# A four-layer graph kernel on one core: the end of layer 1 by quarters of the nodes instead of halves, and another spread of the odd counts

## Chip, cores and metric

The kernel runs on one core of one Trainium2 chip. The metric is the device time of one execution in microseconds (us), the median of the runs shown.

## The reference, cut to what matters

`x` is 4096 nodes by 64 features, `adj` a 4096 x 4096 matrix of zeros and ones. Four layers follow each other, and each adds to `x` what it makes of `h`, the normalised and rectified `x`.

```python
h = jnp.maximum(_layernorm(x, axis=-1), 0.0)
x = x + _L1_gnn_ref(h, adj, ...)      # layer 1
...
# inside _L1_gnn_ref: all pairs of nodes, then work by node
support_t = jnp.einsum('ij,ijd->id', adj_att, x_local)
return proj(expmap(x, support_t, c), c)
...
# _L2_gnn_ref
h_neigh = (adj @ X + X) / deg
z = jnp.concatenate([X, h_neigh], axis=1) @ W + b
out = jax.nn.relu(z); return out / jnp.maximum(norm(out), L2_EPS)
...
# _L3_gnn_ref: the last 100 neighbours of a node, each weighted half of the next
rank = jnp.cumsum(mask, axis=1)
pos = rank - (deg - k)
w = mask * jnp.where(pos > 0, DECAY ** (k - pos), 0.0)
out = w @ (input @ weight) + bias
```

Layer 0 (graph attention with several heads) is not touched by the change.

## The kernel before, in words

**Nodes and tiles.** The 4096 nodes are 32 blocks of 128 (`NB = 32`); `x` and `h` are tiles of 128 partitions by 32 blocks by 64 features. A group is 4 blocks (`GB = 4`, 512 nodes), and there are 8 groups (`NG`). A half is 16 blocks, a quarter 8.

**Who sets the order.** The kernel is recorded through a tile layer. A planner orders the instructions of each engine's queue by costs of its own and keeps the data dependencies; every engine then works its queue strictly in order, and a wait blocks all that stands behind it. Two means pin that order. `in_order()` (lines 921 to 940) ties all instructions of VectorE, ScalarE and TensorE recorded inside it to the one recorded ahead on the same engine. `tc.issue_after(i)` lets the planner place what is recorded inside only behind instruction `i`.

**Odd counts.** `count_odd` (line 946) loads 1 MB of the adjacency into one of two `raw` buffers (SP's queue, line 949) and counts on VectorE the entries that are neither 0 nor 1 (line 950). There are 64 of these. They feed a flag that chooses the general kernel at the end, and nothing else, so they may stand anywhere; they are spread over the layers. This text calls them counts.

**Layer 1, pairs** (`pairs_fast`, from line 2130). For 36 pairs of groups, two to a batch, weights (`sg`), distances (`at`, `xt`) and their transposes (`pf`) are made, and TensorE adds up `accj` and `acci` (line 2280) in PSUM. VectorE adds each finished group to `VT` (lines 2311, 2312, 2338). The last batches are (7,0),(7,1); (7,2),(7,3); (7,4),(7,5); (7,6),(7,7): the columns of groups 0 and 1 are final three batches ahead of the end.

**Layer 1, end by node** (`finish_steps`, line 2356, then `norm_steps`, line 959, and `nodes`, line 2495). For a run of blocks TensorE turns `VT` back (`pvt`, line 2376) and VectorE scales it into `VQ` (2380). Then some 14 wide steps over nodes by 64 features (`xv`, `xu`, `xg`, `V`, ..., `hs`) and some 30 small ones over nodes alone follow on VectorE, with ScalarE between: a square (`vv`), Sqrt (`un`), Tanh (`arg`), Sqrt (`pp`), the norm's square and Sqrt, and two copies into `HH` (lines 2499, 2506), the high and low parts of `h` that layer 2 multiplies by. Sqrt and Tanh need different tables, and a table load (`ACT_TABLE_LOAD`) stands ahead of each change. The steps are Python generators: a `yield True` marks a wait for ScalarE. `side_by_side` runs half 0 and takes, at each such mark, up to two steps of half 1 (ten in all); the whole stands in `in_order`.

**Layer 2** (from line 2594). For each half `hf` of the target nodes, 8 steps `q` load 1 MB of the mask (`m2`, line 2601, three buffers); TensorE multiplies 16 times for `nacc` (line 2606, needs `HH` of four blocks) and 16 times for `dc` (line 2619, the degrees, needs no `HH`). After a half VectorE and ScalarE copy the sums out (`ev`, `cf`), and four groups go one by one through `layer2_group` (line 2546): `pnf`, `cat`, `tr`, `pz`, `zt`, `nrm`, the norm, `tr`, `psup`, `lo`. Half 1's groups run beside half 2's multiplications. Here `half 1` and `half 2` are `hf = 0` and `hf = 1`.

**Layer 3** (from line 2649). Four passes `u` of 1024 target nodes; in each, 32 blocks `j`: per block TensorE makes the ranks (`pv`, lines 2675 and 2683), ScalarE the weights as powers of two (`w3b`, line 2692), TensorE the sums (`sacc`, line 2657). Masks of 0.5 MB (`m3`, line 2668) come through SP's queue, where the counts' loads stand too. Half 2's groups of layer 2 run beside pass `u = 0`; the counts of layer 3 are held until the last of them (`valued[-1]`).

**Where the counts stand before.** 16 in layers 0 and 1; in layer 2, behind the last node step (`ready[-1]`), `q = 5, 6, 7` of half 1 and `q = 0` to `4` of half 2, that is 8; in layer 3 seven in `u = 0` and 11 in each later pass, that is 40.

Of the kernel before, what the change touches and what calls it, by code (L numbers as in the profile page):

```python
# [9 lines left out]
F32 = mybir.dt.float32  # L10
# [14 lines left out]
P = 128  # L25
N = 4096
NB = N // P
D = 64
G = 512
NG = N // G  # L30
GB = G // P
JT = 4
NQ = NB // JT
# [20 lines left out]
HB = NB // 2  # L54
# [776 lines left out]
def kernel(  # L831
# [66 lines left out]
    halves = [slice(b, b + NB // 2) for b in range(0, NB, NB // 2)]  # L898
# [57 lines left out]
    def small(name, width=NB):  # L956
        return spool.tile([P, width], F32, name=name, tag=name)

    def norm_steps(bs, wide, tag, act=True):


        nb = bs.stop - bs.start
        hb = h[:, bs]
        mean = small(f"ln_mean{nb}", nb)
        nc.vector.tensor_reduce(mean, x[:, bs], AX.X, ALU.add)
        yield False
        nc.vector.tensor_scalar(mean, mean, 1.0 / D, None, ALU.mult)
        nc.vector.tensor_tensor(hb, x[:, bs], over(mean, D), ALU.subtract)
        yield False
        sq = wide.tile([P, nb, D], F32, name="ln_sq", tag=tag)  # L970
        if act:
            nc.scalar.activation(sq, hb, AF.Square)
        else:
            nc.vector.tensor_tensor(sq, hb, hb, ALU.mult)
        yield act
        var = small(f"ln_var{nb}", nb)
        nc.vector.tensor_reduce(var, sq, AX.X, ALU.add)
        nc.scalar.activation(var, var, AF.Sqrt, bias=eps_t, scale=1.0 / D)
        yield True
        nc.vector.reciprocal(var, var)  # L980
        nc.vector.scalar_tensor_tensor(hb, hb, 0.0, over(var, D), ALU.max, ALU.mult)
        yield False

    def layernorm_relu(pool=None, tag="wide"):
        with ExitStack() as ln:
            wide = pool or ln.enter_context(tc.tile_pool(name="ln", bufs=2))
            for bs in halves:
                for _ in norm_steps(bs, wide, tag, act=pool is None):
                    pass

    def side_by_side(first, second, fill, most):


        for wait in first:
            for _ in range(min(fill, most) if wait else 0):
                next(second)
                most -= 1
        for _ in second:
            pass

    def transpose_to(dst, src, cols, pool, engine_copy):

# [40 lines left out]
    with ExitStack() as l0:  # L1043
# [260 lines left out]
        with ExitStack() as pa:  # L1304
# [3 lines left out]
            ps = pa.enter_context(tc.tile_pool(name="ps_prep", bufs=2, space=PSUM))  # L1308
# [1044 lines left out]
                if n + 2 < len(batches):  # L2353
                    distances(batches[n + 2])

    def finish_steps(hf, VQ, VT, fold_v, pabs, f, f2, kp, pf, ac2, wide, ps):

        bs = halves[hf]
        n = bs.stop - bs.start
        V, hb, ab = VQ[:, bs, 0:D], h[:, bs], a[:, bs]

        def scal(name):
            return small(name, n)

        def fat(name):
            return wide.tile([P, n, D], F32, name=name, tag="fat")  # L2370

        for g in range(hf * NG // 2, (hf + 1) * NG // 2):
            pt = ps.tile([P, GB, D1], F32, name="pvt", tag="misc")
            for b in range(GB):
                c = (g * GB + b) * P
                nc.tensor.matmul(
                    pt[:, b, :], lhsT=VT[:, c : c + P], rhs=fold_v, start=True, stop=True
                )
            gs = slice(g * GB, (g + 1) * GB)
            nc.vector.tensor_tensor(VQ[:, gs, :], pt, over(pabs[:, gs], D1), ALU.mult)  # L2380
            yield g % 2 == 0
        t = fat("xv")
        nc.vector.tensor_tensor(t, hb, V, ALU.mult)
        yield False
        xu = scal("xu")
        nc.vector.tensor_reduce(xu, t, AX.X, ALU.add)
        yield False
        g = scal("fing")
        nc.vector.scalar_tensor_tensor(g, xu, m2c, VQ[:, bs, D], ALU.mult, ALU.add)
        nc.vector.tensor_tensor(g, g, pinv[:, bs], ALU.mult)  # L2390
        t = fat("xg")
        nc.vector.tensor_tensor(t, hb, over(g, D), ALU.mult)
        yield False
        nc.vector.tensor_tensor(V, V, t, ALU.subtract)
        t = fat("vv")
        nc.scalar.activation(t, V, AF.Square)
        yield True
        nc.vector.tensor_tensor(g, g, ab, ALU.mult)
        nc.vector.tensor_tensor(xu, xu, g, ALU.subtract)
        nc.vector.tensor_tensor(xu, xu, f[:, bs], ALU.mult)  # L2400
        uu, un, arg = scal("uu"), scal("un"), scal("arg")
        nc.vector.tensor_reduce(uu, t, AX.X, ALU.add)
        nc.vector.tensor_tensor(uu, uu, f2[:, bs], ALU.mult)
        nc.vector.tensor_scalar(un, uu, MIN_NORM, None, ALU.max)
        nc.scalar.activation(un, un, AF.Sqrt)
        yield True
        nc.vector.tensor_tensor(arg, un, kp[:, bs], ALU.mult)
        nc.scalar.activation(arg, arg, AF.Tanh)
        nc.vector.reciprocal(un, un)
        yield True  # L2410

        nc.vector.scalar_tensor_tensor(arg, un, rabs, arg, ALU.mult, ALU.mult)
        nc.vector.tensor_tensor(uu, uu, arg, ALU.mult)
        nc.vector.tensor_tensor(uu, uu, arg, ALU.mult)
        nc.vector.tensor_tensor(xu, xu, arg, ALU.mult)
        num, den, one2, pp = scal("mnum"), scal("mden"), scal("one2"), scal("pp")
        nc.vector.tensor_scalar(one2, xu, p2c, 1.0, ALU.mult, ALU.add)
        nc.vector.tensor_tensor(den, ac2[:, bs], uu, ALU.mult)
        nc.vector.tensor_tensor(den, den, one2, ALU.add)
        nc.vector.tensor_scalar(den, den, MIN_NORM, None, ALU.max)  # L2420
        nc.vector.scalar_tensor_tensor(pp, xu, 2.0, ab, ALU.mult, ALU.add)
        nc.vector.tensor_tensor(pp, pp, uu, ALU.add)
        nc.vector.tensor_tensor(pp, pp, den, ALU.mult)
        nc.vector.tensor_scalar(pp, pp, 1e-36, None, ALU.max)
        nc.scalar.activation(pp, pp, AF.Sqrt)
        nc.vector.scalar_tensor_tensor(num, uu, cc, one2, ALU.mult, ALU.add)
        nc.vector.reciprocal(den, den)
        nc.vector.tensor_tensor(arg, arg, pf[:, bs], ALU.mult)
        yield True

        nc.vector.reciprocal(pp, pp)
        nc.vector.scalar_tensor_tensor(den, pp, maxn, den, ALU.mult, ALU.min)
        nc.vector.tensor_tensor(arg, arg, den, ALU.mult)
        nc.vector.tensor_tensor(num, num, den, ALU.mult)
        nc.vector.tensor_tensor(V, V, over(arg, D), ALU.mult)
        yield False
        t = fat("xn")
        nc.vector.tensor_tensor(t, hb, over(num, D), ALU.mult)
        yield False
        nc.vector.tensor_tensor(V, V, t, ALU.add)  # L2440
        yield False
        nc.vector.tensor_tensor(x[:, bs], x[:, bs], V, ALU.add)
        yield False
        yield from norm_steps(bs, wide, "fat")


    VALH = float(1 << 12)
    VBITS = 128.0

    def layers_fast(es, *sums):  # L2450
        HO2 = N // 4
        NK = HO2 // G
        cp = es.enter_context(tc.tile_pool(name="lconst", bufs=1))
# [10 lines left out]
        cnt16 = cp.tile([P, 2, G], BF16, name="cnt16")  # L2464

        ps = es.enter_context(tc.tile_pool(name="ps_l23", bufs=2, space=PSUM))
        wide = es.enter_context(tc.tile_pool(name="finwide", bufs=3))
        lp = es.enter_context(tc.tile_pool(name="l2f", bufs=1))
        work = es.enter_context(tc.tile_pool(name="l2fwork", bufs=2))
        w2 = lp.tile([2 * D, D], F32, name="w2f")  # L2470
# [21 lines left out]
        )  # L2492
        ready, valued = [], []

        def nodes(hf):
            yield from finish_steps(hf, *sums, wide, ps)
            bs = halves[hf]
            hs = wide.tile([P, HB, D], F32, name="hs", tag="fat")
            nc.scalar.activation(HH[:, bs, 0, :], h[:, bs], AF.Copy, scale=VALH)
            yield True  # L2500
            ready.append(
                nc.vector.scalar_tensor_tensor(
                    hs, h[:, bs], VALH, HH[:, bs, 0, :], ALU.mult, ALU.subtract
                )
            )
            nc.scalar.activation(HH[:, bs, 1, :], hs, AF.Copy, scale=LO)


        with in_order():
            side_by_side(nodes(0), nodes(1), 2, 10)  # L2510

        def not_before_nodes():
            return tc.issue_after(ready[-1].ins)
# [81 lines left out]
        with tc.tile_pool(name="ps_nacc", bufs=6, space=PSUM) as ps_acc:  # L2595
            for hf in range(2):
                accs = [ps_acc.tile([P, G], F32, name="nacc", tag="nacc") for _ in range(NS)]
                dc = ps_acc.tile([P, G], F32, name="dc", tag="nacc")
                for q in range(NQ):
# [3 lines left out]
                    for t in range(JT):  # L2603
                        j = q * JT + t
                        for k in range(NS):
# [4 lines left out]
                                start=(j == 0),  # L2610
                                stop=(j == NB - 1),
                            )
                    if q <= NQ // 2 if hf else q > NQ // 2:
                        with not_before_nodes():
                            count_odd(work, next(todo))
                    for t in range(JT):
# [34 lines left out]
        for u in range(4):  # L2651
# [14 lines left out]
            for q in range(NQ):  # L2666
                m = work.tile([P, JT, HO2], U8, name="m3", tag="m3", bufs=3)
                nc.sync.dma_start(m, mask_d[q][u // 2][:, :, hs])
                for t in range(JT):
# [20 lines left out]

                    w = work.tile([P, HO2], I16, name="w3b", tag="w3b", bufs=3)
                    nc.scalar.activation(w, pv, AF.Relu)  # L2692
                    if j % 3 == 0 if u else j % 2 and j > NB // 2 + 1:
                        with tc.issue_after(valued[-1].ins):
                            count_odd(work, next(todo))
                    if last is not None:
# [27 lines left out]
    with tc.If(general == 0):  # L2724
        with ExitStack() as es:
            vp = es.enter_context(tc.tile_pool(name="vq", bufs=1))
            VQ = vp.tile([P, NB, D1], F32, name="VQ")


            VT = vp.tile([P, N], F32, name="VT")  # L2730
# [17 lines left out]
            nc.vector.reciprocal(kp, pm)  # L2748
            nc.vector.tensor_scalar(kp, kp, sqc, None, ALU.mult)
            nc.vector.tensor_scalar(ac2, a, c2, None, ALU.mult)  # L2750
            layers_fast(es, VQ, VT, fold_v, pabs, f, f2, kp, pf, ac2)
        nc.vector.tensor_reduce(bad[:, 0:1], bad, AX.X, ALU.add)
        odd = spool.tile([P, 1], F32, name="odd")
        nc.gpsimd.partition_all_reduce(odd, bad[:, 0:1], P, RMAX)
# [58 lines left out]
```

## Time and profile before

| what | us |
|---|---|
| median of 3 runs (lowest, highest) | 2209.63 (2207.31, 2216.82) |
| the profiled execution | 2209.57 |
| its span | 2207.8 |
| TensorE busy in the span | 1907.8 (86%) |
| VectorE busy | 1753.9 (79%) |
| ScalarE busy | 1600.9 (73%) |
| `raw` loads, from issue to landing, median | 7.0 |

Times in the rows of a profile are from the start of the span. PE is TensorE, PEld its weight loads, DVE VectorE, ACT ScalarE, POOL GpSimd and SP the engine that issues most transfers; a `q` behind the name means its queue. A row of a timeline gives start, duration, engine, line, operation, what is written and read with the shapes, and the count; in brackets stands how long the engine was idle ahead of it, and what ended that. `raw<-in_adj_dram` is the load of a count. A row of waits gives who waited for whom, with the sum in us, the number of times and the longest. Matmuls are pipelined, so their durations overlap: the distance between starts tells the rate. The granted clock is a share of TensorE's full clock.

### The profile page before, as it was taken

What the parts mean: (1) busy time and instruction counts of PE and PEld (TensorE: products, weight loads), DVE (VectorE), ACT (ScalarE), POOL (GpSimd) and SP (SyncE); (2) the same over time, 40 slices, a digit from 0 to 9 for tenths busy, and PEclk for the clock granted to TensorE, in tenths of its full rate; (3) what the DMA queues carried; (4) which work ended last, traced back from release to release, by engine and by line L of the source; (5) the groups of instructions that cost most, each with busy time, mean ns of one, the idle gap of its engine ahead of it and who ended that gap; (6) DMA issues with size and microseconds to landing.
All of it is one profiled execution on the core that took longest, in us unless ns stands there. A gap on an engine that the chain in (4) does not pass through costs nothing.

```text
span 2207.8 us, 43777 instructions
## 1 busy us (share of the span) xinstructions
PE 1907.8 (86%) x19276; PEld 862.1 (39%) x19276; DVE 1753.9 (79%) x2151; ACT 1600.9 (73%) x1359; POOL 84.4 (4%) x124
## 2 busy tenths in 40 slices
PE   4989989999999999938993689999999983989877
PEld 3444444444444444423442323333333331444222
DVE  6689989997898899978766698998989878534555
ACT  3678878997798799846882678888888953137545
POOL 1000100000000000001110000000000000000000
PEclk8999999999999999959996789999999996979989
DMA  9945554353111111078551101110110013803887
GB/s 111 187 94 97 101 78 112 126 188 121 45 45 45 45 50 50 15 254 313 175 190 30 34 15 34 34 34 20 33 39 29 29 50 143 332 31 126 307 311 259
DMA packets 117008, 239.01 MB, mean 108 GB/s; under 512 B 11059, under 2 KB 84003, under 8 KB 102051
## 3 DMA queue, kind: packets, MB, share of 16 engines
q1 hardware_dynamic: 101990, 192.92, 25.4%
q0 software_dynamic: 14816, 43.18, 11.2%
q8 instruction: 153, 2.51, 0.5%
q14 instruction: 49, 0.40, 0.1%
HBM read 245.34 MB, written 49.46 MB: 134 GB/s over the span
## 4 chain that ended last, share of the span: by engine, by line
PE 30%; DVE 15%; issue 11%; ACT 6%; DMA 2%; POOL 0%; DVEq 0%; POOLq 0%; ACTq 0%; SPq 0%
PE accj L2280 6%; PE acco L1971 4%; PE pu L2247 3%; PE pl L2216 2%; PE pf L2318 2%; DVE at L2269 2%; PE pl L2219 2%; PE accC L1544 2%; DVE at L2274 1%; PE accB L1544 1%; PE nacc L2606 1%; ACT sg L2203 1%; PE ddo L1984 1%; ACT xt L2203 1%; DMA raw<-in_adj_dram 1%
## 5 line engine op out<-in xcount | busy, mean ns | idle before, releaser
L1208 ACT ACTIVATE st<-srow,nt 128x2048 int8<-128x2048 f32 x352 | 682.8, 1994 | 80.3 <-DVE B L1214 79.5
L1214 DVE TENSOR_TENSOR B<-st,mres 128x1024 int32<-128x1024 int32 x256 | 311.9, 1221 | 70.6 <-PE accC L1544 46.8
L1544 PE MATMUL accB<-B,ybh 128*32 128x512 fp8e4 x3072 | 339.7, 385 | 14.4 <-DVE B L1214 14.4
L1544 PE MATMUL accD<-B,ybh 128*32 128x512 fp8e4 x2048 | 301.9, 388 | 23.6 <-DVE h L1660 23.6
L1544 PEld LDWEIGHTS <-ybh 128*32 128x32 bf16 (+1 forms) x6656 | 196.8, 98 | 239.0 <-issue 76.9
L1544 PE MATMUL accC<-B,ycn 128*32 128x512 fp8e4 x2272 | 268.2, 381 | 1.2 <-issue 1.2
L1544 PE MATMUL accC<-mres,ych 128*32 128x512 fp8e4 x2272 | 268.4, 381 | 0.0
L1544 PE MATMUL accL<-B,ybh 128*32 128x512 fp8e4 x1536 | 220.5, 390 | 4.6 <-DVE h L1664 4.5
L2280 PE MATMUL accj<-sg,VQ 128*64 128x512 f32 (+1 forms) x512 | 198.7, 618 | 18.7 <-DVE VT L2338 7.1
L1544 PEld LDWEIGHTS <-ych 128*32 128x32 f16 x4096 | 169.0, 99 | 116.0 <-issue 10.8
L950 DVE SCALAR_TENSOR_TENSOR raw<-raw 128x2048 f32<-128x2048 f32 x64 | 146.4, 2289 | 82.8 <-DMA raw<-in_adj_dram 82.8
L1202 DVE TENSOR_SCALAR st<-srow,nt 128x2048 uint8<-128x2048 f32 x160 | 205.5, 1285 | 2.5
L2280 PE MATMUL acci<-sg,VQ 128*64 128x512 f32 (+1 forms) x512 | 198.1, 618 | 0.0
L2203 ACT ACTIVATE sg<-pl,rb 128x512 f32<-128x512 f32 x256 | 163.6, 684 | 47.2 <-PE pl L2219 43.0
L2692 ACT ACTIVATE w3b<-pv 128x1024 int16<-128x1024 f32 x128 | 129.6, 1023 | 81.0 <-PE pv L2683 79.9
L1208 ACT ACTIVATE st<-srowo,nto 128x1024 int8<-128x1024 f32 x128 | 137.3, 1137 | 40.7 <-DVE B L1214 40.5
L2247 PE MATMUL pu<-XAf,LDf 66*128 66x512 f32 x288 | 147.5, 615 | 8.6 <-DVE at L2254 7.4
L1544 PE MATMUL accC<-C,ych 128*32 128x512 fp8e4 x1824 | 147.8, 392 | 0.8 <-DVE C L1222 0.8
L1222 DVE TENSOR_TENSOR C<-B,mres 128x1024 int32<-128x1024 int32 x114 | 139.6, 1225 | 3.6
L1544 PEld LDWEIGHTS <-ycn 128*32 128x32 f16 x2272 | 107.6, 97 | 64.4 <-issue 3.6
L2254 DVE TENSOR_SCALAR at<-pu 128x512 f32<-128x512 f32 x144 | 95.3, 685 | 28.8 <-PE pu L2247 28.2
L2216 PE MATMUL pl<-nm,noid 128*128 128x512 fp8e4 x256 | 100.6, 393 | 9.3 <-ACT sg L2203 8.9
(499 smaller groups left out, 3062.1 us busy)
## 6 DMA issues: line engine op xcount, KB each, us to landing
raw<-in_adj_dram SPq DMA_DIRECT2D x64, 1024.0 KB, 7.0
mo<-edges SPq DMA_DIRECT2D x32, 512.0 KB, 4.6
noedge<-nmo POOLq DMA_DIRECT2D x32, 512.0 KB, 4.4
nm<-noedge SPq DMA_DIRECT2D x64, 256.0 KB, 3.0
m<-edges SPq DMA_DIRECT2D x16, 1024.0 KB, 6.3
m<-edges SPq DMA_DIRECT2D x32, 512.0 KB, 6.9
srow<-srow_d SPq DMA_DIRECT2D x15, 1024.0 KB, 7.1
mres<-in_adj_dram POOLq DMA_DIRECT2D x8, 1024.0 KB, 36.6
```

What stands on the lines that cost most here:

```text
L950: nc.vector.scalar_tensor_tensor(raw, raw, 0.0, raw, ALU.is_gt, ALU.not_equal, accum_out=bad[:, c : c + 1])
L1202: nc.vector.tensor_scalar(st[:, i, :].bitcast(U8), srow, negs[:, i : i + 1], EDGE, ALU.is_gt, ALU.mult)
L1208: nc.scalar.activation(st[:, i, :], srow, AF.Sign, bias=negs[:, i : i + 1], scale=-1.0)
L1214: nc.vector.tensor_tensor(B.bitcast(I32), st.bitcast(I32), edges.bitcast(I32), ALU.bitwise_and)
L1222: nc.vector.tensor_tensor(C.bitcast(I32), B.bitcast(I32), edges.bitcast(I32), ALU.bitwise_xor)
L1544: ins = nc.tensor.matmul(acc[k * O : (k + 1) * O, :], lhsT=values, rhs=moving(k), start=start, stop=stop,)
L2203: tc.keep_in_program_order(nc.scalar.activation(*args, **kw))
L2216: nc.tensor.matmul(pl, lhsT=noid, rhs=nm[:, b, :].bitcast(F8), start=True, stop=False)
L2247: nc.tensor.matmul(pu, lhsT=LD[:, j * P : (j + 1) * P], rhs=XA[:, grp(gi)], start=True, stop=True,)
L2254: nc.vector.tensor_scalar(at[:, b, :], pu, UMIN, None, ALU.max)
L2280: nc.tensor.matmul(acc[r : r + n, :], lhsT=XQ[:, src, cols], rhs=w, start=start, stop=stop)
L2692: nc.scalar.activation(w, pv, AF.Relu)
```

## The change

The end of layer 1 goes by four quarters in place of two halves. `finish_steps` takes a slice of blocks, its small tiles come from the pool `wide` (two buffers to a name), and that pool is opened ahead of the pairs, so that the space of a quarter's tiles is not that of the pairs. Each quarter takes, at its waits for ScalarE, up to two steps of the next (seven in all, two of them the groups' `pvt`). No mark for a wait stands at the groups' steps any more. The nodes' steps stand in `in_order` as before; nothing ties them to the end of the pairs but data and buffers.

The counts: layer 2 takes `q = 5, 6, 7` of half 1 and all eight of half 2 (11 in place of 8); layer 3 takes ten in `u = 0` and nine in each later pass (37 in place of 40). They are still held until the last node step and until the last group of layer 2.

```diff
-    def side_by_side(first, second, fill, most):
-        for wait in first:
-            for _ in range(min(fill, most) if wait else 0):
-                next(second)
-                most -= 1
-        for _ in second:
-            pass
...
-    def finish_steps(hf, VQ, VT, fold_v, pabs, f, f2, kp, pf, ac2, wide, ps):
-        bs = halves[hf]
+    def finish_steps(bs, VQ, VT, fold_v, pabs, f, f2, kp, pf, ac2, wide, ps):
         n = bs.stop - bs.start
...
         def scal(name):
-            return small(name, n)
+            return wide.tile([P, n], F32, name=name, tag=name)
...
-        for g in range(hf * NG // 2, (hf + 1) * NG // 2):
+        for g in range(bs.start // GB, bs.stop // GB):
...
-            yield g % 2 == 0
+            yield False
...
-        wide = es.enter_context(tc.tile_pool(name="finwide", bufs=3))
...
+        QB = NB // 4
+        def nodes(bs):
+            yield from finish_steps(bs, *sums, wide, ps)
+            hs = wide.tile([P, QB, D], F32, name="hs", tag="fat")
...
+        quarters = [nodes(slice(b, b + QB)) for b in range(0, NB, QB)]
         with in_order():
-            side_by_side(nodes(0), nodes(1), 2, 10)
+            for quarter, after in zip(quarters, quarters[1:] + [iter(())]):
+                most = 7
+                for wait in quarter:
+                    for _ in range(min(2, most) if wait else 0):
+                        next(after, None)
+                        most -= 1
...
-                    if q <= NQ // 2 if hf else q > NQ // 2:
+                    if hf or q > NQ // 2:
                         with not_before_nodes():
                             count_odd(work, next(todo))
...
-                    if j % 3 == 0 if u else j % 2 and j > NB // 2 + 1:
+                    if (j % 7 < 2 and j < 28 or j == 30) if u else j % 3 and j > NB // 2:
                         with tc.issue_after(valued[-1].ins):
                             count_odd(work, next(todo))
...
+            wide = es.enter_context(tc.tile_pool(name="finwide", bufs=2))
...
-            layers_fast(es, VQ, VT, fold_v, pabs, f, f2, kp, pf, ac2)
+            layers_fast(es, wide, VQ, VT, fold_v, pabs, f, f2, kp, pf, ac2)
```

More of the change, by code (lines that the diff above doesn't have):

```diff
@@ L963, in norm_steps @@
         hb = h[:, bs]
-        mean = small(f"ln_mean{nb}", nb)
+        mean = small("ln_mean", NB // 2)[:, 0:nb]
         nc.vector.tensor_reduce(mean, x[:, bs], AX.X, ALU.add)
@@ L975, in norm_steps @@
         yield act
-        var = small(f"ln_var{nb}", nb)
+        var = small("ln_var", NB // 2)[:, 0:nb]
         nc.vector.tensor_reduce(var, sq, AX.X, ALU.add)
@@ L2448, with layers_fast @@
     VBITS = 128.0
-    def layers_fast(es, *sums):
+    def layers_fast(es, wide, *sums):
         HO2 = N // 4
@@ L2493, in layers_fast @@
         ready, valued = [], []
[L2495 to L2498, printed above, removed]
+        QB = NB // 4
+        def nodes(bs):
+            yield from finish_steps(bs, *sums, wide, ps)
+            hs = wide.tile([P, QB, D], F32, name="hs", tag="fat")
             nc.scalar.activation(HH[:, bs, 0, :], h[:, bs], AF.Copy, scale=VALH)
```

## The prediction

> **What bounds the kernel now.** The profiled execution took 2209.57 us, 1.8 more than its span and 0.1 under the median of the runs shown, so a sum made against it holds for the median too. I read first the busy times by stage (columns: window, length, busy PE, PEld, DVE, ACT and POOL with counts, granted TensorE clock, DMA share, GB/s).
>
> ```profile
> 1784.00:1818.00 34.00, 29.88 (x180) 14.44 (x180) 23.44 (x30) 16.83 (x17) 3.62 (x7) 1.00 0.12 42
> 1818.00:1854.00 36.00, 0.00 (x0) 0.00 (x0) 30.04 (x65) 13.08 (x16) 0.74 (x2) 0.50 0.45 153
> 1854.00:1890.00 36.00, 34.66 (x227) 13.61 (x228) 23.98 (x44) 3.90 (x7) 0.00 (x0) 0.93 0.61 221
> 1890.00:1926.00 36.00, 34.69 (x249) 17.66 (x248) 23.59 (x44) 7.12 (x17) 2.54 (x3) 1.00 0.86 318
> 1926.00:1963.00 37.00, 29.43 (x197) 18.19 (x194) 13.98 (x38) 9.64 (x23) 1.41 (x3) 0.84 0.19 73
> 1963.00:2031.00 68.00, 65.81 (x322) 28.40 (x320) 25.25 (x64) 46.82 (x70) 0.80 (x2) 0.91 0.22 65
> 2031.00:2087.00 56.00, 48.59 (x228) 17.30 (x227) 32.36 (x36) 34.00 (x34) 1.56 (x2) 0.97 0.87 305
> 2087.00:2147.00 60.00, 45.09 (x177) 13.32 (x176) 32.21 (x28) 28.75 (x30) 1.49 (x2) 0.89 0.92 324
> 2147.00:2203.00 56.00, 48.09 (x230) 17.31 (x229) 31.99 (x36) 34.88 (x36) 3.38 (x5) 1.00 0.77 273
> ```
>
> The rows are: the last pair sums (VectorE idle 10.6 of 34); the end of layer 1, with TensorE idle throughout; layer 2 (half 1 to 1893, then half 2 to 1963), TensorE nearly full; layer 3, passes u=0 to u=3. In u=1 and u=2 the DMA share is 0.87 and 0.92. Next the timelines of TensorE, VectorE and ScalarE.
>
> ```profile
> 1854.06 5.91 PE L2606 MATMUL nacc<-m,HH 128*128 128x512 fp8e4 x16 [36.67 <-ACT HH L2506]
> ...
> 1860.88 3.63 PE L2606 MATMUL nacc<-m,HH 128*128 128x512 fp8e4 x16
> ```
> ```profile
> 1819.15 1.22 DVE L2386 TENSOR_REDUCE xu<-xv 128x16 f32<-128x1024 f32 x1
> ...
> 1890.47 2.29 DVE L950 SCALAR_TENSOR_TENSOR raw<-raw 128x2048 f32<-128x2048 f32 x1 [7.18 <-DMA raw<-in_adj_dram]
> ...
> 1897.79 0.43 DVE L2558 TENSOR_TENSOR cat<-cat,degf 128x256 f32<-128x256 f32 x1
> ```
> ```profile
> 1831.80 1.28 ACT L2408 ACT_TABLE_LOAD   x1
> 1833.09 0.21 ACT L2408 ACTIVATE arg<-arg 128x16 f32<-128x16 f32 x1
> ```
>
> TensorE waits 36.67 us for the first half of the nodes. The second half is done at 1871.4 (VectorE's `hs` ends at 1870.3, then ACT's copy of 1.06), while TensorE still works on the first. So from 1854.06 TensorE bounds half 1 of layer 2, up to its last `nacc` at 1893.5. Last, the waits between 2087 and 2147, and SP's queue there.
>
> ```profile
> DVE raw L950 <- DMA raw<-in_adj_dram: 24.4, 14, 4.9
> ...
> PE pv L2683 <- DMA m<-edges: 8.5, 6, 2.8
> ```
> ```profile
> 2126.46 0.62 SPq L2668 DMA_DIRECT2D m<-edges  x1
> 2132.58 3.01 SPq L949 DMA_DIRECT2D raw<-in_adj_dram  x2
> 2135.68 0.52 SPq L2668 DMA_DIRECT2D m<-edges  x1
> ```
>
> Layer 3's masks stand behind pairs of odd counts in one queue. A count's load waits until one of two `raw` buffers is free, so TensorE waits for counts that it doesn't use.
>
> **Part 1, quarters.** A half has 14 wide VectorE steps of 1.22 (1.26 from start to start) and some 5.6 us of small ones: 23.2. Between the rows of 1024 elements (1.26) and 256 (0.46) one of 512 comes to 0.73; the small ones hardly shrink. A quarter costs 14 x 0.73 + 5.6 = 15.8. Four are 63.2, two halves 46.5: **16.7 us more** VectorE work. The built program's order on each engine, read beside the old one, puts 8.3 us of it ahead of the last VT step: quarter 0 up to `un`, and quarter 1's `xv`, `xu`, `xg`. That fits the 10.6 idle, here and there 0.4 late. On TensorE the order puts `pvt` of two groups (1.00 each) ahead of the last eight sums, where 0.8 was idle: +1.2. If that cover fails, all 8.3 is paid (rival 3).
>
> After the last VT step (ended 1815.3, now 1816.9) I walk VectorE's new order. Left are 63.2 - 8.3 + 1.5 (`VQ` of two quarters) + 0.7 (`cf`, now ahead of the last `ln_var`) = 57. Waits come to 8: per quarter for Tanh, whose load (1.28) can start only after the quarter ahead has its last `HH` (0.85), and for `HH`'s first half (0.65); in the last quarter also for `ln_sq` and `ln_var` (1.0), since no quarter follows to fill them; and for `cf`, which waits for TensorE's third quarter (1.2). So `hs` ends at about 1881.7, and `HH` is whole at about 1831, 1849, 1867 and **1882.3**: the first nodes 23 us earlier, the last 11 later.
>
> By then TensorE has 96 of half 1's 128 `nacc` and all its `dc` behind it; 32 follow. They cost 32 x 0.222 = 7.1 (3.63 per 16, less the tail), `pm` 0.3, and a restart from idleness, 5.91 - 3.63 = 2.3: the last is at 1892.0, for 1893.5 before. **Gain 1.4.** The 23 us early start leaves nearly nothing, since the last nodes are late next.
>
> The Trainium skill ("TensorE: Matmul & The Clock Gate", Part 1) says that an idle window of about 3.4 us halves the clock and about 3.4 us of work restores it, so a restart loses 1.7; by that the sum would be 0.6 better. The row loses 2.3 (clock 0.50, then 0.93), and I keep it. The skill's "ScalarE: Activation LUTs" (What ACT_TABLE_LOAD costs) gives 2.66 us for a switch with its drain, which speaks against quarters: nine loads stand in the new order, for five. By that the sum would be some 4 us worse. Here, though, the activation starts 0.01 after a load of 1.28.
>
> **Part 2, layer 2's counts.** Eight were here, now 11; VectorE reaches the first at 1885, not 1873.5, since it is held until the last nodes. Four stood in the node groups' serial chain, now nine. From one `pnf` end to the next the chain took 16.6 and 15.5 (two counts each), 13.9 (none), and 11.4 to the last `tr`. So two counts cost 1.6 to 2.7. By place: nothing behind `cat` while TensorE transposes; about 1.3 behind `zt`, where 0.93 was idle; all 2.3 between `recip` and `h`. With the new places (4, 2, 2 and 1 per group) I get 17.5, 16.5, 15.0 and 11.9, **3.5 longer**; 1.2 earlier at its start, the chain has its last `tr` at 1957.0, **2.3 later** than 1954.67. Layer 3 starts behind it in the same order as before, so it moves by 2.3.
>
> Unknown is how long a count's load takes to land. I take 7.0, the page's median for `raw`; the one issued at 1881.3 took 9.1 (the 1890.47 row). Between free buffer and use I find 7.3 for two of the counts and 8.2 for a third: at 9.1 these add about 2, 2 and 1, and the chain behind them a little, together +6. The queue has 9 counts and 7 masks of 1.05 MB to bring in 46 us, 365 GB/s where 318 was shown, so that end stays in the range. The other end is nothing.
>
> **Part 3, layer 3's counts.** Of 40 that ran here 37 remain. In u=1 and u=2 they go at 4.36 us each (35 between 2031.6 and 2184.2). If they set the pace to the end, 3 x 4.36 = 13 goes. But u=3 runs at 1.31 us a block from 2151 on, nearly TensorE's six matmuls (6 x 0.215): there they hold up nothing. The new order puts 25 counts, not 26, ahead of u=2's last mask, which is then issued at 2133.0, not 2135.7: 2.7. One mask wait in u=3 goes, 1.3. The last `ev` no longer stands behind a count (2195.1 to 2197.4): 0.9. **Gain 4.9**, between 0 and 13; I take the u=3 rows as nearest.
>
> Sum: 2209.6 + 2.3 - 4.9 = **2207.0** (the 1.4 is in the chain's start). A difference under 0.5%, 11 us, is about what a measurement of this kernel cannot tell from no change.
>
> **Rivals.**
> 1. The counts pace layer 3 to its end, and layer 2 loses nothing: 2209.6 - 13 = 2196.6. For it: shares of 0.87 and 0.92. Against: 0.77 and clock 1.00 in u=3. Chance 0.17, faster.
> 2. Slower: the loads in layer 2's second half land late inside VectorE's ordered chain (the 6 on top of 2.3), and a TensorE that idles for them restarts once more (2.3); layer 3's masks keep their old pace: 2209.6 + 8.3 + 2.3 = 2220. It decides from a landing of about 7.3 us on. For it: 318 GB/s there already. Against: VectorE's long wait of before hurt nobody. Chance 0.20, of which 0.12 beyond 0.5%.
> 3. The first quarter isn't beside the sums: its steps push them by all 8.3 instead of 1.2: 2207 + 7 = 2214. Against: VectorE's idle gaps of 0.8, 2.4 and 1.9 stand where the steps are put. Chance 0.08.
>
> My forecast has the other 0.55. **Chances:** faster 0.17, within 0.5% 0.55 + 0.08 + 0.08 = 0.71, slower 0.12. The range goes from rival 1, 2196, to nearly rival 2, 2219.
>
> **What would show it.** The first `nacc` starts near 1831, not 1854, yet half 1's last ends near 1892, after a last `HH` near 1882. The chain from the first `pnf` to the last `tr` takes 61 us, not 57. u=3 still takes about 45 us. I am wrong if the last quarter ends before 1875, if the sums end over 3 us later, or if u=1 to u=3 shrink by over 10.

## The result, and the profile after

The changed kernel took 2207.70 us (median of 20 runs, 2200.23 to 2215.85), the kernel before 2215.12 in 20 runs beside it (its three runs shown above had 2209.63). The ratio is 0.9972, with a 95% interval of 0.9958 to 0.9987: 6.2 us faster, between 2.9 and 9.3. Measured once more (12 runs of the changed kernel beside 17 of the one before), the ratio was 0.9981 (0.9967 to 0.9994), 4.2 us. The forecast was 2207.0, "within 0.5%", 2.6 us faster. The profiled execution took 2203.01.

Executions of one program differ by several us ahead of the change already. So the marks below are counted from the fifth VectorE addition into `VT` from the end of the pairs (1763.54 in the profile before, 1764.64 in the one after): up to it the two programs keep the same distances. "Chain" is from the start of the first `pnf` of half 1's four groups, which go one after the other beside half 2's multiplications, to the start of the fourth group's last `tr`; "layer 3" is from that `tr` to the end of VectorE's last step.

| us from the mark | first `pnf` | last `tr` | chain | layer 3 |
|---|---|---|---|---|
| before | 132.7 | 191.1 | 58.5 | 246.5 |
| after | 126.4 | 191.2 | 64.8 | 238.9 |
| after, executed once more | 126.5 | 191.3 | 64.8 | 244.1 |

All of the gain is in layer 3. Ahead of it the chain starts 6.3 earlier and is 6.4 longer. Busy times by stage of the kernel after (columns: window, length, busy PE, PEld, DVE, ACT, POOL with counts, granted TensorE clock, DMA share, GB/s):

```profile
1784.00:1818.00 34.00, 29.42 (x173) 12.93 (x169) 30.59 (x51) 22.28 (x25) 3.62 (x7) 1.00 0.10 25
1818.00:1831.00 13.00, 0.00 (x0) 0.00 (x0) 10.51 (x36) 3.33 (x8) 0.74 (x2) 0.53 1.01 409
1831.00:1882.00 51.00, 40.83 (x248) 18.09 (x249) 38.86 (x124) 16.99 (x28) 0.61 (x1) 0.80 0.40 140
...
2031.00:2087.00 56.00, 49.88 (x239) 17.86 (x238) 33.41 (x36) 35.35 (x37) 1.97 (x3) 1.00 0.90 311
2087.00:2147.00 60.00, 48.65 (x199) 15.30 (x198) 33.68 (x31) 31.19 (x32) 1.09 (x2) 0.89 0.93 332
2147.00:2201.00 54.00, 43.24 (x203) 14.51 (x200) 23.74 (x28) 32.09 (x32) 3.39 (x5) 0.94 0.60 215
```

Beside the last pair sums VectorE now has 30.59 of 34 us of work (23.44 before). TensorE stands for 13 us in the second row, where it stood for 36 before. In u=1 and u=2 the DMA shares are as high as before; in u=3 the share has fallen from 0.77 to 0.60. TensorE's timeline, kernel after:

```profile
1831.02 0.61 PE L2603 MATMUL nacc<-m,HH 128*128 128x512 fp8e4 x1 [16.45 <-ACT HH L2497]
...
1875.93 1.05 PE L2616 MATMUL dc<-m,sel 128*32 128x512 fp8e4 x16 [1.34 <-DMA m<-edges]
1879.46 5.73 PE L2603 MATMUL nacc<-m,HH 128*128 128x512 fp8e4 x18 [2.49 <-DMA m<-edges]
1885.12 0.43 PE L2531 MATMUL pm<-wsq,ones 64*128 64x64 f32 x2
1885.49 4.92 PE L2603 MATMUL nacc<-m,HH 128*128 128x512 fp8e4 x22
1890.25 0.95 PE L2631 MATMUL pdeg<-qsel,cf 128*128 128x4 f32 x8
1891.06 1.08 PE L2549 MATMUL pnf<-fold_h,ev 128*128 128x64 f32 x8
```

The first `nacc` waits 16.45, not 36.67, and the last of half 1 ends at about 1890.2. New are waits for masks (`DMA m`). Eight of the 18 `nacc` from 1879.46 belong to half 2's first step, which needs only the first quarter's nodes: they stand ahead of the last `HH` (1881.7) and run through the slow restart of the clock that the forecast gave to half 1's last 32.

### The profile page after: what moved, and what is told of

Its sections match the earlier page's. It is cut to its first block, busy times and chain, and to the rows that moved or that the text cites. A ratio compares the mean times of both kernels' runs of the same rounds, so it can differ in the third digit from the quotient of the medians.

```text
span 2201.3 us, 43889 instructions
## 1 busy us (share of the span) xinstructions
PE 1916.3 (87%) x19276; PEld 865.8 (39%) x19276; DVE 1763.7 (80%) x2239; ACT 1608.9 (73%) x1379; POOL 85.5 (4%) x124
## 4 chain that ended last, share of the span: by engine, by line
PE 33%; DVE 16%; ACT 6%; DMA 5%; issue 4%; POOL 0%; DVEq 0%; SPq 0%; POOLq 0%; ACTq 0%
PE accj L2270 6%; PE acco L1961 4%; DMA raw<-in_adj_dram 4%; PE pu L2237 3%; PE pl L2206 2%; DVE raw L950 2%; PE pf L2308 2%; DVE at L2259 2%; PE pl L2209 2%; PE accC L1534 2%; PE nacc L2603 1%; ACT st L1198 1%; DVE at L2264 1%; PE accB L1534 1%; ACT sg L2193 1%
## 5 line engine op out<-in xcount | busy, mean ns | idle before, releaser
L2270 PE MATMUL accj<-sg,VQ 128*64 128x512 f32 (+1 forms) x512 | 199.5, 620 | 17.9 <-DVE sg L2311 7.0
L1534 PEld LDWEIGHTS <-ycn 128*32 128x32 f16 x2272 | 107.5, 97 | 62.5 <-issue 1.5
```

The lines of the kernel that those rows point to most:

```text
L1534: ins = nc.tensor.matmul(acc[k * O : (k + 1) * O, :], lhsT=values, rhs=moving(k), start=start, stop=stop,)
L2270: nc.tensor.matmul(acc[r : r + n, :], lhsT=XQ[:, src, cols], rhs=w, start=start, stop=stop)
```

## The experiments

**Theory T**, as it stood after the two traces: the quarters start the chain earlier, the counts pushed into it give that back, and the net gain is what fewer counts ahead of masks save in layer 3. **R1**: the counts do it all, the quarters nothing. **R2**: the counts pace layer 3 to its end, each at 4.36. All marks at once; ratios are to the kernel before, beside it on the same chip. Rows 1 to 4, 5 to 8, 9 to 11 and 12 come from four chips, with medians of the kernel before of 2211.73, 2211.43, 2212.70 and 2211.03; each median of a row stands on 12 runs or on 6. The last four columns are from one execution each.

| kernel | median us | ratio (95%) | first `pnf` | last `tr` | chain | layer 3 |
|---|---|---|---|---|---|---|
| quarters, old spread | 2214.70 | 1.0022 (1.0005 to 1.0039) | 126.4 | 188.8 | 62.4 | 255.0 |
| halves, new spread | 2207.73 | 0.9984 (0.9970 to 0.9999) | 132.7 | 195.2 | 62.5 | 240.7 |
| after, `cf` behind the nodes | 2211.39 | 1.0001 (0.9986 to 1.0017) | 126.3 | 195.8 | 69.4 | 241.8 |
| after, pool behind the pairs | 2206.36 | 0.9980 (0.9966 to 0.9993) | 127.1 | 191.6 | 64.5 | 242.1 |
| after, six counts of u=3 out | 2201.90 | 0.9957 (0.9942 to 0.9973) | 126.3 | 191.1 | 64.9 | 238.0 |
| after, six of u=1, u=2 out | 2194.37 | 0.9918 (0.9901 to 0.9936) | 126.3 | 191.1 | 64.8 | 231.2 |
| after, u=0's counts early | 2197.92 | 0.9938 (0.9921 to 0.9954) | 126.3 | 195.8 | 69.5 | 226.9 |
| after, once more | 2207.55 | 0.9981 (0.9967 to 0.9994) | 126.5 | 191.3 | 64.8 | 244.1 |
| before, three buffers | 2193.65 | 0.9916 (0.9898 to 0.9935) | 132.7 | 190.6 | 58.0 | 233.9 |
| quarters, old spread, three buffers | 2196.13 | 0.9924 (0.9906 to 0.9943) | 126.8 | 191.4 | 64.7 | 237.3 |
| after, three buffers | 2206.82 | 0.9966 (0.9949 to 0.9983) | 126.3 | 196.2 | 69.9 | 239.4 |
| halves, three buffers, counts even | 2188.85 | 0.9894 (0.9876 to 0.9912) | 132.7 | 190.7 | 58.0 | 233.2 |

**The changed kernel once more.** The same file.

> The changed kernel once more. Every theory: the same as on record, 4 to 9 us faster than the kernel before (ratio 0.996 to 0.999), and its trace repeats the steps within 1 us (last HH near 1881.7, last tr near 1955.9), which tells how far one execution's rows can be trusted.

In the first `pnf` and the last `tr` the two executions agree within 0.05 us (the last `HH` is 0.2 apart); in layer 3 they are 5.3 apart. So a row ahead of layer 3 can be trusted to some 0.2 us where TensorE's clock runs alike, and a single layer 3 only to some 5 us: for layer 3 the medians count.

**The quarters alone.** After, with

```diff
-                    if hf or q > NQ // 2:
+                    if q <= NQ // 2 if hf else q > NQ // 2:
...
-                    if (j % 7 < 2 and j < 28 or j == 30) if u else j % 3 and j > NB // 2:
+                    if j % 3 == 0 if u else j % 2 and j > NB // 2 + 1:
```

> The quarters of the changed kernel with the old spread of counts in layers 2 and 3 (8 and 40). Theory T (the quarters start half 2's chain of node groups about 5 us earlier, and the added counts of layer 2 give that back; the net gain of the change is layer 3's three counts): the chain keeps its old length of 57 to 58 from the first pnf to the last tr, the last tr is 4 to 6 us earlier than before, near 1949, and the whole is 3 to 6 us faster than before. Rival R1 (the spread of the counts gives all, the quarters nothing): within 1.5 us of before, the last tr near 1954. Prediction on record: half 1 ends 1.4 us earlier, so 1 to 2 us faster.

**The new spread alone.** Before, with the same two conditions the other way round.

> The kernel before with the new spread of counts alone (11 in layer 2, 37 in layer 3). Theory T: the chain of half 2's groups becomes 6 us longer (about 64 for 57), so layer 3 starts 5 to 6 us later, and layer 3 gains 6 to 7: the whole within 2 us of before. Rival R1 (the counts give all): 5 to 7 us faster than before. Prediction on record: 3.5 lost in the chain, 4.9 gained in layer 3, so 1 to 2 us faster.

The row that opens and the row that ends each chain, quarters alone, then counts alone (start, duration, engine, line, operation):

```profile
1887.95 1.08 PE L2549 MATMUL pnf<-fold_h,ev 128*128 128x64 f32 x8
...
1950.36 1.03 PE L995 MATMUL tr<-ident,h 128*64 128x128 f32 x4 [5.83 <-DVE h L981]
```
```profile
1894.91 1.08 PE L2552 MATMUL pnf<-fold_h,ev 128*128 128x64 f32 x8
...
1957.43 1.03 PE L1005 MATMUL tr<-ident,h 128*64 128x128 f32 x4 [6.62 <-DVE h L981]
```

1950.36 - 1887.95 = 62.4 and 1957.43 - 1894.91 = 62.5, where before had 58.5. Each part alone makes the chain 4 longer; together 6.4. By group (from one `pnf` to the next, the fourth to its last `tr`), with the number of counts that VectorE works in each:

| kernel | group 1 | group 2 | group 3 | group 4 | counts |
|---|---|---|---|---|---|
| before | 16.6 | 15.5 | 13.9 | 12.5 | 2, 2, 0, 0 |
| quarters, old spread | 18.0 | 18.2 | 13.9 | 12.3 | 4, 2, 0, 0 |
| halves, new spread | 16.6 | 15.5 | 17.9 | 12.6 | 2, 2, 3, 0 |
| after | 18.0 | 18.2 | 15.3 | 13.3 | 4, 2, 2, 1 |

The quarters alone push two more counts into the chain. Counts are held until the last node step, which comes later, and the chain starts earlier, so only two of layer 2's eight are done ahead of it, not four. Group 1 then has four (kernel with the quarters alone):

```profile
1891.16 2.29 DVE L950 SCALAR_TENSOR_TENSOR raw<-raw 128x2048 f32<-128x2048 f32 x1 [1.05 <-DMA raw<-in_adj_dram]
...
1894.18 2.28 DVE L950 SCALAR_TENSOR_TENSOR raw<-raw 128x2048 f32<-128x2048 f32 x1
...
1900.93 2.26 DVE L950 SCALAR_TENSOR_TENSOR raw<-raw 128x2048 f32<-128x2048 f32 x1
...
1903.45 2.28 DVE L950 SCALAR_TENSOR_TENSOR raw<-raw 128x2048 f32<-128x2048 f32 x1
```

Group 2 has two counts in both kernels and is 2.7 longer with the quarters. Of this 1.4 lies ahead of `zt` (6.1 from `pnf`, for 4.7), where TensorE ran at a clock of 0.74 and 0.83 over 8 us:

```profile
1908.15 1.08 PE L995 MATMUL tr<-ident,cat 128*128 128x128 f32 x4 [0.64 <-DVE cat L2555]
```

That `tr` took 0.60 at full clock before. Another 1.6 lies between `zt` and `h`, where the counts now stand behind `zt` and ahead of `h` instead of behind `cat` and beside ScalarE's square; 0.4 comes back after that. What made the clock drop there was not tested.

The quarters start the chain 6.3 earlier, so alone they win 2.3 up to the last `tr`; the counts alone lose 4.0. The quarters' win ahead of layer 3 had the expected sign and half the size, and the whole went against theory T: slower than before by 1 to 9 us, since layer 3 took 255.0 for 246.5, with the same order of instructions on SP, VectorE and ScalarE there. The new spread alone came out 0.2 to 6.6 us faster: its layer 3 gained 5.8, and it lost 4.0 ahead of it. On the whole time R1 comes nearest: the gain is with the counts, though smaller than the 5 to 7 it asked for, and the quarters alone lose instead of giving nothing. On the stages R1 fails, since without the quarters the last `tr` comes 4 later.

**`cf` behind the last node step.** In the profile after, VectorE stands inside the last quarter for the degrees:

```profile
1877.02 0.69 DVE L2624 COPY cf<-dc 128x512 f32<-128x512 f32 x1 [2.96 <-PE dc L2616]
```
```diff
-                nc.vector.tensor_copy(cf, dc)
+                with not_before_nodes():
+                    nc.vector.tensor_copy(cf, dc)
```

> The changed kernel with the copy cf, in which VectorE waits 2.96 us for TensorE within the last quarter's steps, held until behind the last node step. Theory (that wait sits on the chain that ends the last quarter): the last HH comes 2.5 to 3.5 us earlier, near 1878.5, half 1's last nacc and the last tr as well by 1 to 3 us, and the whole is 1 to 3 us faster than the changed kernel. Rival (TensorE is itself late with its mask loads, so the last nacc ends where it did): the last HH is earlier, the last nacc and the end are within 1 us.

The last `HH` came 2.8 earlier from the mark (114.2 for 117.0), the first `pnf` 0.1: the rival holds, TensorE is late with its masks. But the last `tr` came 4.5 later and the whole some 4 slower than the changed kernel by the medians (2211.39 to 2207.55), which nobody expected. The stretch 1924 to 1935 of TensorE alone, in this kernel and then in the kernel after (columns: window, length, busy PE, clock, DMA share, GB/s):

```profile
1924.00:1935.00 11.00, 10.42 (x37) 0.53 0.55 198
```
```profile
1924.00:1935.00 11.00, 9.99 (x72) 1.00 0.80 287
```

Half the clock for 10 us, behind a wait of 2.20 for `h`. In the kernel after, TensorE waits 2.21 for the same `h` and keeps the full clock.

**The pool behind the pairs.** After, with `finwide` opened in `layers_fast`.

> The changed kernel with the pool of the quarters' tiles opened behind the pairs, as before, so that the first quarter's steps can reuse space of the pairs only once they are done. Theory (8.3 us of the quarters' VectorE work is hidden beside the last pairs' sums only because the pool lies ahead): first nacc 5 to 9 us later than 1831, the last HH near 1888 to 1890, the whole 5 to 8 us slower than the changed kernel. Rival (what counts is that four quarters overlap each other and TensorE; the place beside the sums is worth nothing): within 1.5 us of the changed kernel.

The first `nacc` came 1.5 later, the last `HH` 0.7, the whole no different. The trace shows that the cover was hardly taken away: the first quarter's `xv` starts at 1806.5 instead of 1789.4, as space of the pairs comes free, still ahead of the sums' end at 1812. So this tells what the place of the pool is worth (0.7), not what the cover is worth.

**Counts left out of u=3, and of u=1 and u=2.** `if u == 3 and j in (0, 7, 14, 15, 21, 22)`, or `u in (1, 2) and j in (0, 14, 21)`: a memset of the flag's column instead of the count.

> The changed kernel with six of the nine counts of pass u=3 of layer 3 left out (their column of the flag is set to zero instead, so those parts of the adjacency are not examined). Theory T (in u=3 TensorE sets the pace and the counts hold up nothing): 0 to 2 us faster than the changed kernel. Rival R2 (the counts pace layer 3 to its end at 4.36 us each): 20 to 26 us faster.

> The changed kernel with three of the nine counts of u=1 and three of u=2 left out (their column of the flag is set to zero instead, so those parts of the adjacency are not examined). Theory T (a count ahead of the masks of u=1 and u=2 costs 2 to 2.4 us, its share of the load queue, because TensorE waits for masks behind it): 9 to 14 us faster than the changed kernel. Rival R2 (4.36 us each): 20 to 26 faster. Rival R3 (layer 3's pace is set by TensorE everywhere and the gain in layer 3 is something else): 0 to 3 faster.

Six counts of u=3 were worth 5.6 by the medians; u=3 itself went from 46.6 to 44.0 (from `ev` to `ev`). That is 0.4 to 0.9 each: not free, so theory T was too low with its 0 to 2, and far from R2's 4.36. Six of u=1 and u=2 were worth 13.2, 2.2 each, as theory T had it. R2 falls, R3 too.

**u=0's counts early.**

```diff
-                        with tc.issue_after(valued[-1].ins):
+                        with tc.issue_after(valued[-1 if u else NS].ins):
```

> The changed kernel with the ten counts of u=0 held only until half 2's first node group of layer 2, not its last. Theory T (the queue and VectorE have room in u=0, where the DMA share is 0.2 to 0.4, and counts moved up there come off the masks of u=1): 2 to 8 us faster than the changed kernel, if the last tr stays within 1 us. Rival (VectorE's counts stand in the groups' serial chain): last tr 4 us or more later and no gain.

9.6 us faster than the changed kernel, more than the 2 to 8 of theory T, though the last `tr` came 4.5 later (the second group took 20.1 for 18.2 and the third 18.1 for 15.3, as with `cf` behind the nodes) and u=0 took 91 us for 76. The late `tr` is not the rival's doing: through the chain VectorE, ScalarE and SP have the same rows in the same order as in the changed kernel. What differs is TensorE's clock, from this `tr` of the second group on (this kernel, then the kernel after):

```profile
1921.62 1.03 PE L995 MATMUL tr<-ident,h 128*64 128x128 f32 x4 [2.20 <-DVE h L981]
```
```profile
1924.99 0.60 PE L995 MATMUL tr<-ident,h 128*64 128x128 f32 x4 [2.21 <-DVE h L981]
```

What paid was u=1 to u=3, with 44.1, 44.0 and 44.3. TensorE is busy nearly throughout there, and no wait for a mask is left from 2050 on:

```profile
2085.00:2150.00 65.00, 64.81 (x313) 22.24 (x311) 37.44 (x40) 48.49 (x49) 2.98 (x4) 1.00 0.93 332
```

So 44 is TensorE's own time for a pass. The changed kernel has 49, 64 and 46.6, some 27 us more. In its trace TensorE waits 8.3 there for masks and 11.6 for `w3b`, which ScalarE makes from `pv`, and u=2 runs at a clock of 0.89; how much of the 27 each brings was not taken apart.

**Three buffers.** In u=2 of the kernel before, two counts and a mask go in some 8.4 us: a load lands 5.1 to 7.9 us after its issue, and the next one for that buffer waits until the count (2.3) is done. Now and then little is under way meanwhile (DMA share 0.41 from 2100 to 2101, 0.16 from 2132 to 2133). Theory P took that loop for the pace, rival B the bytes.

```diff
-        raw = pool.tile([P, HW], F32, name="raw", tag="raw", bufs=2)
+        raw = pool.tile([P, HW], F32, name="raw", tag="raw", bufs=bufs)
```

with `bufs` 3 in layers 2 and 3.

> The kernel before with three raw buffers in layers 2 and 3. Theory P: layer 3 (238 from its first pv) becomes 6 to 14 shorter, the whole 4 to 12 us faster than before. Rival B: within 2 us, or up to 8 slower.

> The quarters with the old spread of counts and three raw buffers in layers 2 and 3. With two buffers the quarters began layer 3 2.4 us earlier and yet ended 3 us later than before. Theory P (that loss is a worse phase of the two-buffer loop: 9.0 us for two counts and a mask, not 8.4, in the same order of instructions): with three buffers the loop has slack, and this kernel is 1 to 4 us faster than the kernel before with three buffers. Rival (the loss belongs to the quarters or to where their pool puts the buffers in memory): it stays 2 to 7 us slower than the kernel before with three buffers.

> The changed kernel with three raw buffers for the counts of layers 2 and 3 in place of two. Theory P (layer 3's pace is the loop of two buffers: a load of some 7 us and a count of 2.3 give two counts per 8.4 to 9 us, with DMA engines idle a tenth of the time): a count costs less, the DMA share of u=1 and u=2 goes from 0.9 to nearly 1, layer 3 (from its first pv, 231 to 236 us in the changed kernel) takes 222 to 229, and the whole is 4 to 12 us faster than the changed kernel. Rival B (what counts is bytes ahead of a mask in the queue: three loads stand ahead of a mask, not two, and the transfers are at their limit): within 2 us, or up to 8 slower.

By the medians the kernel before gained 19, more than the 4 to 12 of theory P, the quarters with the old spread 18.6 (2214.70 to 2196.13), the changed kernel 1, as rival B had it. So neither theory has the whole. P is right that the third buffer keeps transfers under way: from 2031 to 2085 the DMA share in the kernel before goes from 0.87 to 0.99.

```profile
2031.00:2085.00 54.00, 42.92 (x178) 13.63 (x178) 39.35 (x39) 27.32 (x27) 1.57 (x2) 0.84 0.99 379
```

That stretch is u=1, which by itself gets longer (58.1 for 50.8 before), with 16 loads of counts issued in it instead of 11. The gain is in u=2, 47.9 for 67.3: 11 such loads are issued there instead of 16, and from 2093 to 2188 TensorE waits for no mask (8.5 us from 2087 to 2147 before).

B is right where loads stand in a row. SP's queue at the start of u=1, before with three buffers, then after with three:

```profile
2029.60 21.07 SPq L949 DMA_DIRECT2D raw<-in_adj_dram  x8
2050.77 0.52 SPq L2668 DMA_DIRECT2D m<-edges  x1
```
```profile
2034.59 34.48 SPq L949 DMA_DIRECT2D raw<-in_adj_dram  x11
2069.16 0.52 SPq L2665 DMA_DIRECT2D m<-edges  x1
```

With two buffers a mask stood behind every two loads. With three, the planner puts all counts of u=0 and one more in a row ahead of u=1's next mask: eight where u=0 has seven, eleven where it has ten. TensorE waited for that mask (who waits for whom, sum, times, longest; before with three buffers, then after with three):

```profile
PE pv L2683 <- DMA m<-edges: 8.8, 1, 8.8
```
```profile
PE pv L2680 <- DMA m<-edges: 14.3, 1, 14.3
```

That the quarters would be faster than the halves with three buffers (1 to 4) did not come: 2196.13 to 2193.65, 2.5 slower, as the rival had it (2 to 7), though the intervals overlap.

**Three buffers and counts spread evenly**, on the halves of before:

```diff
-                    if j % 3 == 0 if u else j % 2 and j > NB // 2 + 1:
+                    if j % 8 in (0, 3, 5) if u else j >= NB - 4:
```

> The kernel before (halves) with three raw buffers and layer 3's 40 counts spread anew: four in u=0 and twelve in each later pass, so that six loads, not eight, stand in a row ahead of u=1's third mask (eleven did so in the changed kernel with three buffers, whose u=1 took 67 us; eight in the kernel before with three buffers, 58 us). Theory Q (with three buffers what costs is the row of loads ahead of u=1's masks, some 3 us each at the transfers' limit, and u=1 to u=3 have room for twelve each): u=1 takes 50 to 54, u=2 and u=3 stay at 48 to 50, and the whole is 2 to 8 us faster than the kernel before with three buffers (0.984 to 0.990 of before). Rival (twelve per pass, with masks 16.8 MB in 44 us, is more than the transfers bring, so every later pass gets longer): u=2 and u=3 at 51 or more, no gain.

```profile
2027.34 14.19 SPq L949 DMA_DIRECT2D raw<-in_adj_dram  x6
```

Six in a row, and TensorE waits 1.4 for that mask instead of 8.8. From the end of one pass's last `ev` to the next, u=1 took 50.5 (58.1 with seven in u=0), u=2 and u=3 some 49.2 each (47.9): theory Q. The median is 4.8 lower, 2188.85, though the intervals of the two ratios overlap. This kernel has the lowest median here, and neither the quarters nor the change's spread.

## Why the prediction was nearly right, point by point

**The time** was right within 1 us, the difference was not: 2.6 forecast, 6.2 and 4.2 measured. That the time fits is in part luck. The three runs of before that the sum stands on were 5.5 lower than the median of 20, and that hid a term: layer 3 was to gain 4.9 and what stands ahead to lose 2.3. Ahead nothing was lost (191.2 for 191.1 from the mark), and this too is the sum of two misses: the chain starts 6.3 earlier, not 1.2, and is 6.4 longer, not 3.5. Layer 3 took 241.5 in the mean of the five executions with the new spread and two buffers, 5.0 less than before in its one. The signs of both large terms are shown by the new spread alone (4.0 lost in the chain, 5.8 gained in layer 3). The rivals fell: the counts do not pace u=3 (rival 1), no late load slowed layer 2 by 8 (rival 2), the first quarter's steps moved the sums' end by 0.6 (rival 3).

**Part 1, quarters.** `HH` whole at "1831, 1849, 1867 and 1882.3": 1831.0, 1848.0, 1865.0 and 1881.7. The place beside the sums and the 0.73 for a step of 512 (0.72 measured from start to start) were right; the extra work of 16.7 was a little high (the durations of the node steps sum to 60.2 for 45.2, so 15.0). "**Gain 1.4**" was mis-sized: the last `nacc` came 4.4 earlier from the mark (1893.5 less 1763.54, and 1890.2 less 1764.64), and the first `pnf` 6.3. The term that was mis-sized is "32 follow ... and a restart": counted from the mark the last `HH` was 1.7 earlier than worked out, and half 2's eight `nacc` took part of the restart (8.5 for 9.7). The last 1.8 came from `cf`, which I had counted only as a cost: before, it stood behind `ev` at 1894.55 and held up `pdeg` and `pnf`; inside the last quarter it is long done.

**Part 2, layer 2's counts.** The mechanism was right: nine counts stand in the chain, 4, 2, 2 and 1 by group, as forecast. "**3.5 longer**" was mis-sized; it was 6.4. By group it was to be 0.9, 1.0, 1.1 and 0.5 longer, and was 1.5, 2.7, 1.4 and 0.8. More than half of the 2.9 missed is group 2, where the clock dropped (1.4), which no term had. The kernel with the new spread alone does not test the 3.5, since its counts stand 2, 2, 3 and 0; the three in its group 3 cost 4.0, some 1.3 each. The kernel with the quarters alone shows the part that comes from where the last node step stands: two counts more in group 1 cost 1.5. The bound of +6 for late loads was not needed: in the kernel after, waits for counts inside the chain were below 1 us.

**Part 3, layer 3's counts.** "**Gain 4.9**" held, as a mean. Its reason, that u=2's last mask is issued 2.7 earlier, can't be read from one trace: from the mark it was issued at 368.9 and 374.2 in the two executions after, at 372.1 before. What does show it is the 2.2 us of a count in u=1 and u=2, and the lengths of the passes: in the five executions with the new spread and two buffers u=2 took 63.1 to 65.5 for 67.3 in the one before, and u=3 46.2 to 47.1 for 48.7, on the mean 2.6 and 2.1 less, where the forecast had 2.7 and 2.2. "There they hold up nothing", of u=3, is too strong: 0.4 to 0.9 each. And the value is no property of the spread: with three buffers the same new spread is 11 us slower than the old one (2206.82 to 2196.13, both with quarters), since it puts ten counts in a row ahead of u=1's masks.

**Left open.** Why the quarters with the old spread took 8.5 us longer in layer 3 than before, in the same order of issue. By the medians it is some 5 (3.0 slower in all, though the last `tr` came 2.3 earlier). In the trace most of it is u=3, 54.3 for 48.7: TensorE waits 3.3 there for masks, for which it did not wait before, and its clock is 0.94 for 1.00. What sets the loop's phase was not found. Where the quarters' pool puts the buffers in memory was varied only with the new spread, and made no difference there. Why the clock drops in some groups and not in others is open as well.

## What to carry to other kernels

An early start of a stage is worth only what its last input allows, and less where work that is held until the stage's end then falls into the next stage's serial chain (here two counts): ask what the saved time turns into one stage later. Work that nobody waits for still costs through the queue and the buffers that it shares with work that somebody waits for: count how many of its loads stand in a row ahead of a needed one, and try a third buffer before moving it about (19 us here, against 4 to 6 for the change). Where executions agree to some 0.2 us up to one stage and scatter by 5 in it, judge the first by one trace and the second by medians.

## What the runs showed of the hardware

In the node groups TensorE's clock dropped to half behind waits of 0.64 to 3.28 us (`tr` at 1.03 to 1.08 instead of 0.60), while waits of 0.60 to 0.71 left it whole in the kernel before; what decided it was less than the rows can tell (2.20 and 2.21 above, with the same instructions). It also came back after very different times with the same instructions. The first 20 us of layer 3 on TensorE, counted from the last `tr`, before with three buffers and then with the even spread (columns as in the last two rows of TensorE):

```profile
1957.60:1977.60 20.00, 18.95 (x77) 0.65 0.09 26
```
```profile
1950.80:1970.80 20.00, 18.94 (x65) 0.50 0.00 1
```

Both come out of a wait of 5.83 and are busy for 95%, yet the half clock lasts some 14 us in the one and 24 in the other (to 1971.9 and 1974.5), and the first `ev` of u=0 came 4.7 later in the second, counted from that `tr`. The Trainium skill ("TensorE: Matmul & The Clock Gate", Part 1) has the clock halved after an idle window of about 3.4 us and restored by about 3.4 us of sustained work, with a window that runs freely. The free window agrees with what looks like luck here. The two times do not: none of the waits of 0.64 to 3.28 reached 3.4, and the half clock lasted up to seven times as long, though with small gaps in the work.

A load takes longer beside others: in the kernel before a mask of 0.5 MB took 6.1 to 8.1 us (median 7.2) from issue to landing behind counts in u=2, and 3.9 (median) in u=0, where only masks were loaded. The same skill ("Trainium Kernel Development and Optimization", Best Practices) advises two buffers, to overlap transfers with work; here a third brought the kernel before from a DMA share of 0.87 (2031 to 2085) to 0.99, and 19 us, won one pass later.
